# Attention rows from a v formed once, with blocks of p as the stationary operand

## The chip, the cores and the metric

The kernel runs on one core of a Trainium2 chip, alone. The metric is device time in microseconds (us) of one launch, as a median over runs. All data are float32.

Engines are called as the profile calls them: PE is TensorE (matrix multiply; PEld its weight loads), DVE is VectorE, ACT is ScalarE, POOL is GpSimd, SP is SyncE, which here only issues DMAs. A matmul has a stationary operand, loaded into the array as weights of 128 rows by up to 128 columns, and a moving operand that is streamed through; its result goes to PSUM, of which a bank holds 512 float32 per partition. A float32 matmul appears in the profile as two records.

## The reference, cut to what matters

Two layers over N = 4096 rows. Layer 0 is attention over all rows (width D = 512) with the matrix `adj` added twice to the scores, layer 1 a graph convolution with the same `adj` (hidden width 128). Each is followed by a residual and a layer norm.

```python
q, k, v = x @ Wq.T + bq, x @ Wk.T + bk, x @ Wv.T + bv
a = q @ k.T / sqrt(512) + adj + adj
x1 = layernorm(x + softmax(a) @ v)
h = relu(adj @ (x1 @ W1) + b1)
out = layernorm(x1 + adj @ (h @ W2) + b2)
```

The change concerns `softmax(a) @ v` alone. Because the rows of the softmax sum to one, `softmax(a) @ v = softmax(a) @ (x @ Wv.T) + bv`, which can be computed as `(p @ x) @ Wv.T` or as `p @ (x @ Wv.T)`, p being the exponentials, divided by their row sums at the end.

## The kernel before

The work is laid out by hand: `tc.manual_schedule()` keeps each engine's instructions in the order in which the Python code issues them. Rows of the attention are handled in 8 groups of 512 (`NG`, index g). The scores are held transposed: for group g a tile pair q (16 of them) holds 256 keys by 512 rows of the group.

**Small recursion.** Most products of 512x512 blocks use the Strassen-Winograd form: 7 products of half-sized blocks, in the order 1, 2, 6, 7, 5, 4, 3 (`ORDER`), of sums and differences of quarters (S1 to S4 on one side, T1 to T4 on the other). Products 1, 6, 5, 3 accumulate in one PSUM bank (X), 2, 7, 4 in another (Y), and after each product the bank is read and added to a quarter of the result. So reads are many and small, and a product must not be added to a bank before the previous sum there has been read.

**Stages.**
- Start: M, the product of Wq and Wk, is formed, and u = M x for group 0 (`u_fast(0)`).
- Scores of group 0 (`qk`, read by `qk_read`), with `u_fast` of groups 1 to 7 placed between. Beside them `sum_x` loads x by pairs of tiles, lets GpSimd form four sums of its quarters and stores them in `xs_d`.
- Groups: while `qk` forms the scores of group g+1, the exponentials p of group g are prepared and multiplied with x. This is `px`: for each of 5 blocks of tile pairs (2, 2, 4, 4, 4 pairs) 7 products, called phases.
- Then the convolution (`strassen`, line 1028, and the loop at line 1330) and the output rows.

**Order.** A group of scores is 16 units (`NP`) of 7 steps. In a step TensorE gets two matmuls of `qk` (call them k, j with j = 0 or 1; X and Y have one buffer each, tags "x" and "y"), then `qk_read` if j = 1, then items from the list `todo` as far as their planned microseconds are due. Before all that, the hooks of the step run: `at(unit, step, f)`. A group's px begins near unit `s1 = (g + 1) * NP`, when its scores are complete:

- `turn_max` (s1, step 5) and `spread_max` (s1+1, step 1) give the maximum of each row in every partition (`MB`); `new_max` has accumulated it on VectorE;
- `shift` subtracts it (VectorE, two per pair), `exps` takes the exponential (ScalarE), `px_t2` forms two differences (GpSimd), all at the places listed in `PREP`;
- `sums` adds the exponentials to `LACC` on GpSimd, two adds of 128x512 per pair; `row_sums` turns this by TensorE and reduces it;
- `px_items`: stationary is a block of x (or of its stored sums), moving the quarter of p, 256 columns. Both 128-row halves f of a phase share a bank. During phase 6 `px_t34`, during phase 7 `px_t1` change the quarters of p in place on VectorE. `px_read` adds the bank to `OT`;
- banks of px, u and v come from four buffers with the tag "o"; the stationary x comes from a ring of four buffers `XN`, loaded by `load_x` three phases ahead.

`OT` is (p x) transposed. `row_items(g - 1)` begins in unit s1+1 and places, between the first px items of group g, the row work of group g-1: `rows_out_fast` (28 matmuls with Wv by the 7 products; the last group has `rows_out`, 16 matmuls of 512 columns, placed beside the convolution), then the layer norm (`stats`, `rows_norm`), `project` and `project2` (x1 @ W1 into `t_sb`) and `add_b2` (x1 + b2 to `x1_d`).

Of the kernel before, what the change touches and what calls it, by code (L numbers as in the profile page):

```python
# [18 lines left out]
P = 128  # L19
# [5 lines left out]
def tile_graph_attention_then_gcn(  # L25
# [89 lines left out]
    xs_d = {a: dram.tile([P, 4, b - a, 2 * P], F32, name=f"xs_d{a}") for a, b in BLOCKS}  # L115
# [38 lines left out]
    FAST_V = range(NG - 1)  # L154
    QUARTER = {1: (0, 0), 2: (0, 0), 6: (1, 0), 7: (1, 1), 5: (1, 1), 4: (1, 0), 3: (0, 1)}
    L = {}
    MV, owing = {}, []
    UT, UO, XTS, SA, S, XN, CB, MB, MACC, LACC, O, OT, RL, XR, T = ({} for _ in range(15))
# [158 lines left out]
    def sum_x(q):  # L317

        if q % 5 < 3:
            w = t_sb[:, ts(q % 5, 8), :].rearrange("p (a b) c -> p a (b c)", a=4)  # L320
        else:
            w = xnp.tile([P, 4, 2 * P], F32, tag="xn", name=f"w{q}")
        a11, a21, a12, a22 = (w[:, k] for k in range(4))
        nc.sync.dma_start(
            w.rearrange("p (t a) c -> p t (a c)", t=2),
            x[ts(q // 2, W), :].rearrange("(t j p) d -> j p t d", p=P, t=2)[q % 2],
        )

        def row_part(r):
            if q >= PER // 2:  # L330
                row_parts(q // 2 * PER + q % 2 + 2 * r, w[:, 2 * r : 2 * r + 2].rearrange("p a d -> p (a d)"))

        def add():
            tt = nc.gpsimd.tensor_tensor
            tt(a22, a21, a22, ALU.add)
            tt(a21, a21, a11, ALU.subtract)
            tt(a11, a22, a11, ALU.subtract)
            tt(a12, a12, a11, ALU.subtract)

        def store():  # L340
            a = max(a for a, _ in BLOCKS if a <= q)
            nc.gpsimd.dma_start(xs_d[a][:, :, q - a, :], w)

        T["sum_x", q] = row_part, add, store
# [111 lines left out]
    def sums(g, q):  # L456
        ck = pair(g, q)
        if q == 0:
            LACC[g] = accp.tile([P, W], F32, tag="lacc", name=f"lacc{g}")
            nc.gpsimd.tensor_tensor(LACC[g], ck[:, 0, :], ck[:, 1, :], ALU.add)  # L460
        else:
            for h in range(2):
                nc.gpsimd.tensor_tensor(LACC[g], LACC[g], ck[:, h, :], ALU.add)  # L463


    PHASES = [(g, a, b, k) for g in range(NG) for a, b in BLOCKS for k in ORDER]

    def load_x(n):
        g, a, b, k = PHASES[n]
        pool = xnp2 if n % 4 > 1 else xnp  # L470
        XN[n] = pool.tile([P, b - a, 2 * P], F32, tag="xn", name=f"xn{n}")
        plain = {1: (0, 0), 2: (1, 0), 4: (1, 1)}
        if k in plain:
            t, f = plain[k]
            src = x.rearrange("(d t j p) f -> t p d j f", p=P, t=2, j=2)[t]
            for d in range(a // 2, b // 2):
                nc.sync.dma_start(
                    XN[n][:, 2 * d - a : 2 * d - a + 2], src[:, d, :, ts(f, 2 * P)]
                )
        else:  # L480
            nc.sync.dma_start(XN[n], xs_d[a][:, {6: 0, 7: 1, 3: 2, 5: 3}[k]])
# [24 lines left out]
    def px_read(g, first, k):  # L506

        letter = "PX" if k in (1, 6, 5, 3) else "PY"
        ps = T[letter].rearrange("p (f i) -> p f i", f=2)
        f, i = {1: (0, 0), 2: (0, 0), 6: (1, 0), 7: (1, 1), 5: (1, 1), 4: (1, 0), 3: (0, 1)}[k]  # L510
        to = OT[g][:, 2 * f : 2 * f + 2, ts(i, HW)]

        def go():
            if first and k in (1, 6, 7, 3):
                if g == NG - 1:
                    nc.vector.tensor_copy(to, ps)
                else:
                    nc.scalar.copy(to, ps)
            else:
                nc.vector.tensor_tensor(to, ps, to, ALU.add)  # L520

        px_reads.append((letter, go))
# [9 lines left out]
    def px_items(g):  # L532
        def one(n, q, f):
            _, a, b, k = PHASES[n]

            def go():
                if q == a and f == 0:
                    if n + 3 < len(PHASES):
                        load_x(n + 3)
                    if k in (6, 5, 3, 4):  # L540
                        read_px(("PY",) if k == 4 else ("PX",))
                    if k == 1 and a == 0:
                        OT[g] = rowp.tile([P, ND, W], F32, tag="ot", name=f"ot{g}")
                    if k in (1, 2, 7):
                        T["PX" if k == 1 else "PY"] = bank("o", f"p{n}", 4)
                begins = k in (1, 2, 7) and q == a
                nc.tensor.matmul(  # L547
                    T["PX" if k in (1, 6, 5, 3) else "PY"][:, ts(f, HW)],
                    XN[n][:, q - a, ts(f, P)],
                    quarters(g, q)[{1: 0, 2: 2, 6: 1, 7: 0, 5: 1, 4: 2, 3: 3}[k]],  # L550
                    start=begins and f == 0,
# [3 lines left out]
                if f == 1:  # L555
                    if k == 6:
                        px_t34(g, q)
                    if k == 7:
                        px_t1(g, q)
                    if q == b - 1:  # L560
                        px_read(g, a == 0, k)
# [4 lines left out]
            one(n, q, f)  # L566
            for n, (g_, a, b, k) in enumerate(PHASES)
            if g_ == g
            for q in range(a, b)
            for f in range(2)  # L570
        ]

    def row_sums(g):
        ps = turn(LACC[g], f"l{g}")
        l = small.tile([P, PER], F32, tag="l", name=f"l{g}")
        nc.vector.tensor_reduce(l, ps, AX.X, ALU.add)
        RL[g] = small.tile([P, PER], F32, tag="rl", name=f"rl{g}")
        if g in FAST_V:
            L[g] = l
            nc.vector.scalar_tensor_tensor(RL[g], l, EPS, l, ALU.mult, ALU.mult)  # L580
        else:
            nc.vector.reciprocal(RL[g], l)

    def add_bv(g):
        xr = XR[g]
        for r in range(PER):
            nc.gpsimd.tensor_tensor(xr[:, r, :], xr[:, r, :], bv_t, ALU.add)
            if g in FAST_V:
                nc.scalar.activation(
                    xr[:, r, :], xr[:, r, :], AF.Copy, scale=L[g][:, r : r + 1]  # L590
                )
# [24 lines left out]
    def rows_out(g, r, c):  # L616
        if c == 0 and r == 0:
            read_px()
        if c == 0:
            T["ro"] = mbank(f"x1_{g}_{r}")  # L620
        ps = T["ro"]
        nc.tensor.matmul(  # L622
            ps, OT[g][:, c, ts(r, P)], wv_t[:, c, :], start=c == 0, stop=c == ND - 1
        )
        if c == ND - 1:
            xr = XR[g][:, r, :]
            nc.vector.scalar_tensor_tensor(xr, ps, RL[g][:, r : r + 1], xr, ALU.mult, ALU.add)
            T["norm", g, r] = norm_stats(small, xr)

    def rows_out_fast(g, k, j):  # L630

        ot = OT[g].rearrange("p (f c) (h i) -> p f h c i", f=2, h=2)
        a11, a12, a21, a22 = (ot[:, f, h] for h in range(2) for f in range(2))
        tt = nc.vector.tensor_tensor

        sum_ = (nc.gpsimd if g == NG - 2 else nc.vector).tensor_tensor

        def read(k):  # L640
            ps = T["VX" if k in (1, 6, 5, 3) else "VY"].rearrange("p (j o) -> p j o", j=2)
            h, i = QUARTER[k]
            to = XR[g][:, 2 * h : 2 * h + 2, ts(i, HW)]
            tt(to, ps, to, ALU.add)

        def stats(r):

            mv = small.tile([P, 4], F32, tag="mv", name="mv2").rearrange("p (n s) -> p n s", n=2)
            for n in range(2):
                st = small.tile([P, nc.vector.BN_STATS_DIM], F32, tag="stats", name="stats")  # L650
                nc.vector.bn_stats(st, XR[g][:, r + n, :])
                nc.vector.bn_aggr(mv[:, n], st)
            rstd = small.tile([P, 2], F32, tag="rstd", name="rstd2")
            tt = nc.gpsimd.tensor_tensor
            tt(rstd, mv[:, :, 1], RL[g][:, r : r + 2], ALU.add)
            tt(rstd, rstd, half_t.to_broadcast([P, 2]), ALU.pow)
            sh = small.tile([P, 2], F32, tag="shift", name="shift2")
            tt(sh, mv[:, :, 0], rstd, ALU.mult)
            nc.gpsimd.tensor_scalar(sh, sh, -1.0, None, ALU.mult)
            for n in range(2):  # L660
                T["norm", g, r + n] = sh[:, n : n + 1], rstd[:, n : n + 1]

        if (k, j) == (1, 0):
            read_px()
            T["s3"] = rowp.tile([P, 2, HW], F32, tag="x1t", name=f"s3_{g}")
            sum_(T["s3"], a11, a21, ALU.subtract)
            sum_(a21, a21, a22, ALU.add)
        if j == 0 and k in (1, 2, 7):
            if k != 1 and m_tags[0] == T["v tag"]:
                m_tags.reverse()  # L670
            T["VX" if k == 1 else "VY"] = mbank(f"v{g}_{k}")
            if k == 1:
                T["v tag"] = m_tags[-1]
# [711 lines left out]
```

## Time and profile before

| | us |
|---|---|
| runs | 2302.60, 2301.88, 2300.53 |
| median | 2301.88 |
| span of the profiled execution, first to last instruction | 2301.7 |
| the same execution's busy PE / DVE / POOL / ACT | 2273.5 / 1615.5 / 1016.0 / 402.8 |
| start of `qk` of group 0, and of the first px | 38, 244 |
| start of the last group's px stage, and of the convolution | 1714, 1849 |

The profile is of one execution; its span is the time of the run but for a fraction of a microsecond, so sums are made against 2301.7. [...]

### The profile page before, as it was taken

To read this page: it belongs to the slowest core of one execution; us is meant where nothing else is said; L and a number is where in the kernel's file an instruction comes from. 1 tells how busy PE (TensorE), PEld (TensorE's weight loads), DVE (VectorE), ACT (ScalarE), POOL (GpSimd) and SP (SyncE) were. 2 spreads that over 40 slices of the span, in tenths; PEclk is the share of its full clock that TensorE was granted. 3 is DMA by queue.
4 is the path that set the end of the run, shared out by engine and by line. 5 is a ranking of instruction groups with operands and counts; after the bars stand their busy time and mean duration, and the time that the engine had idled before them with its cause. 6 is when DMAs were issued, how large, how long until landed. Compare 5 with 4: busy or idle time off the path is not lost.

```text
span 2301.7 us, 28624 instructions
## 1 busy us (share of the span) xinstructions
PE 2273.5 (99%) x10744; PEld 1766.8 (77%) x10744; DVE 1615.5 (70%) x2287; ACT 402.8 (18%) x442; POOL 1016.0 (44%) x1007
## 2 busy tenths in 40 slices
PE   9999999999999999999999999999999999999998
PEld 7888788888888888888888888888887843333456
DVE  5676676676667657866776687567657877888864
ACT  2212211131122113111311121122112000000012
POOL 2666454184337425631653274237428830001043
PEclk9999999999999999999999999999999999999999
DMA  6899778567847694777578477947754468999996
GB/s 189 282 308 296 218 220 232 176 189 212 245 132 215 187 256 110 217 210 217 151 215 241 142 214 196 256 117 210 199 185 156 160 240 325 333 347 374 353 382 218
DMA packets 283721, 525.16 MB, mean 228 GB/s; under 512 B 23297, under 2 KB 130561, under 8 KB 282689
## 3 DMA queue, kind: packets, MB, share of 16 engines
q1 hardware_dynamic: 229040, 406.12, 52.2%
q0 software_dynamic: 43296, 103.56, 20.5%
q10 hardware_dynamic: 11248, 13.65, 1.9%
q8 instruction: 86, 1.41, 0.2%
q14 instruction: 51, 0.41, 0.1%
HBM read 475.27 MB, written 46.41 MB: 227 GB/s over the span
## 4 chain that ended last, share of the span: by engine, by line
PE 93%; DVE 3%; DMA 1%; POOL 1%; issue 0%; ACT 0%; POOLq 0%; DVEq 0%
PE p L547 31%; PE X L407 19%; PE b L1028 15%; PE Y L407 14%; PE psu L246 4%; PE v L676 3%; PE acce L1330 2%; PE tps L722 1%; PE ops L1284 1%; DVE s L497 1%; DVE s L502 1%; PE x1ps L713 1%; DMA s_d<-sa 1%; PE x L622 1%; DMA sa<-in_xT_dram 1%; PE psm L831 1%
## 5 line engine op out<-in xcount | busy, mean ns | idle before, releaser
L547 PE MATMUL p<-s,xn 128*128 128x256 f32 x3584 | 895.6, 380 | 6.7 <-DVE s L502 1.9
L547 PEld LDWEIGHTS p<-s,xn 128*128 128x128 f32 x3584 | 677.6, 190 | 108.4 <-DVE s L502 5.8
L407 PE MATMUL X<-ut,sa 128*128 128x256 f32 x1984 | 514.7, 383 | 3.2 <-DVE macc L429 2.2
L463 POOL TENSOR_TENSOR lacc<-lacc,s 128x512 f32<-128x512 f32 x240 | 345.3, 1439 | 204.7 <-ACT s L454 193.9
L407 PEld LDWEIGHTS X<-ut,sa 128*128 128x128 f32 x1984 | 371.1, 191 | 63.9 <-DVE s L420 14.0
L420 DVE TENSOR_TENSOR s<-X,s 128x512 f32<-128x512 f32 x256 | 176.4, 689 | 285.8 <-PE X L407 281.7
L407 PE MATMUL Y<-ut,sa 128*128 128x256 f32 x1408 | 362.1, 380 | 1.9 <-DMA sa<-in_xT_dram 1.9
L407 PEld LDWEIGHTS Y<-ut,sa 128*128 128x128 f32 x1408 | 267.5, 191 | 38.2 <-DVE s L450 2.3
L454 ACT ACTIVATE s<-s 128x1024 f32<-128x1024 f32 x128 | 135.4, 1058 | 794.6 <-DVE s L450 794.6
L429 DVE TENSOR_TENSOR macc<-macc,s 128x512 f32<-128x512 f32 x240 | 254.7, 1061 | 1.2
L420 DVE TENSOR_TENSOR s<-Y,s 128x512 f32<-128x512 f32 x192 | 131.9, 687 | 165.9 <-PE Y L407 165.0
L450 DVE TENSOR_TENSOR s<-s,mb 128x512 f32<-128x512 f32 x256 | 230.0, 907 | 0.7 <-ACT mb L370 0.7
L520 DVE TENSOR_TENSOR ot<-p,ot 128x512 f32<-128x512 f32 x248 | 168.9, 681 | 28.6 <-PE p L547 28.3
L356 POOL DMA_DIRECT2D s<-in_adjT_dram x64 | 84.3, 1317 | 231.9 <-ACT s L351 231.1
L995 DVE TENSOR_TENSOR tt<-ck 128x1024 f32<-128x1024 f32 x112 | 138.4, 1271 | 38.6 <-PE b L1028 32.9
L1028 PE MATMUL b<-tt,st 128*64 128x512 f32 (+1 forms) x768 | 156.1, 541 | 0.0
L351 ACT COPY s<-cb 128x2048 f32<-128x2048 f32 x64 | 121.0, 1891 | 50.7 <-PE p L547 39.8
L490 POOL TENSOR_TENSOR s<-s 128x256 f32<-128x256 f32 x128 | 121.4, 949 | 0.6
L1028 PEld LDWEIGHTS b<-tt,st 128*64 128x64 f32 x768 | 53.9, 137 | 87.8 <-issue 79.4
L491 POOL TENSOR_TENSOR s<-s 128x256 f32<-128x256 f32 x128 | 108.7, 849 | 10.0
L497 DVE TENSOR_TENSOR s<-s 128x512 f32<-128x512 f32 x128 | 112.9, 902 | 0.0
L460 POOL TENSOR_TENSOR lacc<-s 128x512 f32<-128x512 f32 x8 | 10.6, 1323 | 203.4 <-ACT s L454 203.4
(191 smaller groups left out, 2129.3 us busy)
## 6 DMA issues: line engine op xcount, KB each, us to landing
ck<-in_adjT_dram SPq DMA_DIRECT2D x128, 1024.0 KB, 7.4
s<-in_adjT_dram POOLq DMA_DIRECT2D x64, 1024.0 KB, 11.6
sa<-s_d SPq DMA_DIRECT2D x224, 256.0 KB, 5.4
xn<-in_x_dram SPq DMA_DIRECT2D x192, 256.0 KB, 4.5
xn<-xs_d SPq DMA_DIRECT2D x96, 512.0 KB, 5.2
sa<-in_xT_dram SPq DMA_DIRECT2D x168, 256.0 KB, 4.6
xn<-xs_d SPq DMA_DIRECT2D x64, 256.0 KB, 4.0
ut<-u_d SPq DMA_DIRECT2D x49, 256.0 KB, 7.0
```

The costliest lines, as they stand in the source:

```text
L407: nc.tensor.matmul(T["X" if k in (1, 6, 5, 3) else "Y"][:, ts(j, HW)], SA[g, d, a][:, c, j, :], UT[g, b][:, c, :], start=k in (1, 2, 7) an ...
L420: nc.vector.tensor_tensor(ck, ps, ck, ALU.add)
L429: nc.vector.tensor_tensor(MACC[g], MACC[g], ck[:, h, :], ALU.max)
L450: nc.vector.tensor_tensor(ck, ck, MB[g], ALU.subtract)
L454: nc.scalar.activation(ck, ck, AF.Exp, scale=2.0)
L463: nc.gpsimd.tensor_tensor(LACC[g], LACC[g], ck[:, h, :], ALU.add)
L490: nc.gpsimd.tensor_tensor(b12, b12, b11, ALU.subtract)
L497: nc.vector.tensor_tensor(b, b, t2, ALU.subtract)
L520: nc.vector.tensor_tensor(to, ps, to, ALU.add)
L547: nc.tensor.matmul(T["PX" if k in (1, 6, 5, 3) else "PY"][:, ts(f, HW)], XN[n][:, q - a, ts(f, P)], quarters(g, q)[{1: 0, 2: 2, 6: 1, 7: 0 ...
L995: nc.vector.tensor_tensor(t[:, :2], v[:, :, 1], v[:, 0], ALU.subtract)
L1028: nc.tensor.matmul(BK[n][k][ts(half, HH)], lhs, right(u, i, half, b), start=q == 0, stop=q == NP - 1,)
```

## The change

v = x Wv^T is formed once for all 4096 rows, beside the scores of group 0, and its 7 quarter combinations are stored in DRAM (`vs_d`). In px the blocks of p become the stationary operand, and v streams, 256 columns and a 257th that holds a constant (1, -1, 2 or 0, as the seven products need), which yields the row sums of p in the same products. The result is no longer transposed and needs no product with Wv. Gone are `sums`, `row_sums`, `rows_out`, `rows_out_fast`, the sums of x, and the scaling of x by the row sums. Row work of group g-1 (`rows_sum`, `rows_stats`, `rows_norm`) stands in hooks, and px of a group begins one unit later.

```diff
+    def v_fast(d):
...
+                for c in range(2):
+                    nc.tensor.matmul(
+                        X["X" if k in (1, 6, 5, 3) else "Y"][:, ts(j, HW)],
+                        SA[0, d, OPERANDS[k][0]][:, c, j, :],
+                        WV[OPERANDS[k][1]][:, c, :],
...
+    def store_v(d):
+        to = v_place(d)
+        nc.scalar.dma_start(to[:, 0], VW[d][:, 0])
+        nc.scalar.dma_start(to[:, 1:3], VW[d][:, 2:4])
+
+    def sum_v(d):
+        a11, a21, a12, a22 = (VW[d][:, k] for k in range(4))
+        tt = nc.gpsimd.tensor_tensor
+        tt(a22, a21, a22, ALU.add)
+        tt(a21, a21, a11, ALU.subtract)
+        tt(a11, a22, a11, ALU.subtract)
+        tt(a12, a12, a11, ALU.subtract)
+
+    def store_sums(d):
+        nc.gpsimd.dma_start(v_place(d)[:, 3:7], VW[d])
...
     def load_x(n):
         g, a, b, k = PHASES[n]
         pool = xnp2 if n % 4 > 1 else xnp
...
+        XN[n] = pool.tile(
+            [P, b - a, HW + 1], F32, tag="xn", name=f"xn{n}", padded_shape=[P, 4, HW + 1]
+        )
+        place, ones = {1: (0, 1.0), 2: (1, 1.0), 4: (2, 0.0), 6: (3, -1.0), 7: (4, -1.0),
+                       3: (5, 2.0), 5: (6, 0.0)}[k]
+        nc.gpsimd.memset(XN[n][:, :, HW:], ones)
+        nc.sync.dma_start(XN[n][:, :, :HW], vs_d[a][:, place])
...
-        def one(n, q, f):
+        def one(n, r, q):
...
+                    if k in (1, 2):
+                        T[letter, r] = bank("o", f"p{n}_{r}", 4)
                 nc.tensor.matmul(
-                    T["PX" if k in (1, 6, 5, 3) else "PY"][:, ts(f, HW)],
-                    XN[n][:, q - a, ts(f, P)],
-                    quarters(g, q)[{1: 0, 2: 2, 6: 1, 7: 0, 5: 1, 4: 2, 3: 3}[k]],
-                    start=begins and f == 0,
+                    T[letter, r][:, : HW + 1],
+                    quarters(g, q)[{1: 0, 2: 2, 6: 1, 7: 0, 5: 1, 4: 2, 3: 3}[k]][:, ts(r, P)],
+                    XN[n][:, q - a, :],
+                    start=k in (1, 2, 7) and q == a,
...
-            for q in range(a, b)
-            for f in range(2)
+            for r in range(2)
+            for q in range(a, b)
...
+    def rows_sum(g, r):
...
+        if r == 0:
             read_px()
...
+            RL[g] = small.tile([P, PER], F32, tag="rl", name=f"rl{g}")
+            nc.vector.reciprocal(RL[g], OT[g][:, :, 0, HW])
+        for n in range(2):
+            xr = XR[g][:, r + n, :].rearrange("p (f c) -> p f c", f=2)
+            nc.vector.scalar_tensor_tensor(
+                xr, OT[g][:, r + n, :, :HW], RL[g][:, r + n : r + n + 1], xr, ALU.mult, ALU.add
+            )
...
+    def rows_stats(g, r):
+
+        mv = small.tile([P, 4], F32, tag="mv", name="mv2").rearrange("p (n s) -> p n s", n=2)
+        for n in range(2):
+            st = small.tile([P, nc.vector.BN_STATS_DIM], F32, tag="stats", name="stats")
+            nc.vector.bn_stats(st, XR[g][:, r + n, :])
+            nc.vector.bn_aggr(mv[:, n], st)
+        rstd = small.tile([P, 2], F32, tag="rstd", name="rstd2")
+        tt = nc.gpsimd.tensor_tensor
+        nc.gpsimd.tensor_scalar(rstd, mv[:, :, 1], EPS, None, ALU.add)
+        tt(rstd, rstd, half_t.to_broadcast([P, 2]), ALU.pow)
...
         return [
...
+            *w(4), *pro(0), *w(4), *pro(1), *w(2),
+            *pro2(0), *w(2), *pro(2), *w(2), *pro2(1), *w(2), *pro(3), *w(2), *pro2(2), *w(4),
...
-    work[1] = 15, [(0.86, f) for g in range(1, NG) for f in u_fast(g)] + [(0, lambda: owing.pop()())] * 2
+    first = []
+    for d in range(NG):
+        if d:
+            first += [(0.86, f) for f in u_fast(d)]
+        late = [(0.86, f) for f in v_fast(d)]
+        if d:
+            late[4:4] = [(0, lambda d=d: sum_v(d - 1))]
+            late[12:12] = [(0, lambda d=d: store_sums(d - 1))]
+        first += late
...
+    work[1] = NP - 1, first
...
     PREP = [
-        (1, LATE), (2, EARLY), (2, LATE), (3, MID), (4, EARLY), (4, LATE), (5, EARLY), (5, LATE),
+        (1, (2, 3, 4)), (1, (4, 5, 6)), (2, LATE), (3, MID), (4, EARLY), (4, LATE), (5, EARLY), (5, LATE),
...
-            at(s1 + unit, n2, sums, g, q)
             at(s1 + unit, n2, px_t2, g, q)
...
             items = row_items(g - 1, lambda n: [px.pop() for _ in range(n * by)])
-            work[s1 + 1] = NP, items + px[::-1]
-        else:
-            work[s1 + 2] = NP - 1, px
+            px = items + px[::-1]
+            for n in range(4):
+                at(s1 + 1, 3 + n, (rows_sum, rows_stats)[n // 2], g - 1, n % 2 * 2)
+                at(s1 + 2, n, rows_norm, g - 1, n)
+        work[s1 + 2] = NP - 1, px
```

## Prediction

> **What bounds the kernel now.** I read the engine shares first, then the chain that ended last, then one stretch of the middle.
>
> ```profile
> PE 2273.5 (99%) x10744; PEld 1766.8 (77%) x10744; DVE 1615.5 (70%) x2287; ACT 402.8 (18%) x442; POOL 1016.0 (44%) x1007
> ...
> PE 93%; DVE 3%; DMA 1%; POOL 1%; issue 0%; ACT 0%; POOLq 0%; DVEq 0%
> ```
>
> ```profile
> 650.00:850.00 200.00, 199.63 (x948) 174.42 (x947) 141.72 (x201) 42.16 (x41) 98.27 (x91) 1.00 0.71 197
> ```
>
> TensorE is full: 199.6 of 200 us in the middle, and 93% of the chain. VectorE (141.7) and GpSimd (98.3) have room on the average. So work taken off GpSimd (the row sums) is worth nothing directly; what counts is the sum of matmuls and every new place where TensorE waits. From the chain in order of time:
>
> ```profile
> 1080.74 1.73 PE v L676 x8
> ...
> 1294.73 1.73 PE v L676 x8
> ...
> 1852.67 3.63 PE x L622 x8
> ```
>
> Eight records are four matmuls of 256 columns: 0.216 us a record, 0.432 a matmul. The first two rows open `rows_out_fast` of neighbouring groups, so a group lasts 214.0 us. Its matmuls: 224 of qk and 224 of px, 96.8 each, 28 of v, 12.1, project and project2 5.7, three turns 1.3: 212.7. Barely 1.3 is lost to waits.
>
> **The matmuls.** Removed: `rows_out_fast`, 7 x 28 x 0.432 = 84.7; `rows_out` of the last group, 4 x 3.63 = 14.5; eight turns for row sums at 0.44, 3.5. Added: `v_fast`, 8 x 28 x 0.432 = 96.8; one more column in 1792 px matmuls, 774 x 1/256 = 3.0. The sum is -2.9: v is formed in one place instead of eight, not saved. By stages: the first group's scores grow by 96.8, each middle group shrinks by 12.3, the end by 15. Swapping which px operand is stationary costs nothing: as many weight loads of 128 columns (190 ns each, beside the matmuls) as before.
>
> **The first stage.** Scores of group 0 take 181 us of TensorE now, 278 after. Hidden below that: the load of Wv on SP (1 MB, 7.7 us to landing now; issued ahead of the u matmuls that begin at 26 us, used from 44); 32 GpSimd sums of 512 columns for 64 of 256; copies by ScalarE (18% busy) and its two stores of each block, which wait for a VectorE add of 0.68, with only the next copies behind them; GpSimd's store of the sums. 14.7 MB are stored instead of 8.4, but over a longer stretch (DMA share 0.96 from 60 to 250 us now). TensorE loses some 5 us at 224 to 243 us to late `sa` loads and a full queue; with DMA less dense I take -2, bounds -8 and +3.
>
> **The moved rows, where I expect the loss.** Before, row work of group g-1 lay between v matmuls in the unit that starts px of group g. After, px starts a unit later, and in that unit (s1+1) TensorE has only seven steps of qk, while `rows_sum` and `rows_stats` put all their VectorE work at steps 3 to 6, ahead of the qk reads of the same steps. Bank X is single: product 1 of the next block can't start until product 3 has been read. That such a read holds TensorE shows already in the scores before the first px:
>
> ```profile
> 237.16 3.22 PE Y L407 x8
> 240.38 2.17 PE X L407 x8
> ...
> 242.57 0.70 DVE s L420
> 243.28 0.04 issue
> 243.32 1.13 PE X L407 x4
> ```
>
> X starts 0.05 us after its read has ended. VectorE's prices come from its timeline:
>
> ```profile
> 1313.36 0.70 DVE L651 BATCH_NORM_STATS2 stats<-xr 128x6 f32<-128x512 f32 x1
> 1314.09 0.18 DVE L652 BATCH_NORM_AGGREGATE mv<-stats 128x2 f32<-128x6 f32 x1
> 1314.18 0.66 DVE L651 BATCH_NORM_STATS2 stats<-xr 128x6 f32<-128x512 f32 x1
> 1314.88 0.18 DVE L652 BATCH_NORM_AGGREGATE mv<-stats 128x2 f32<-128x6 f32 x1
> 1314.98 0.66 DVE L450 TENSOR_TENSOR s<-s,mb 128x512 f32<-128x512 f32 x1
> 1315.56 0.68 DVE L420 TENSOR_TENSOR s<-X,s 128x512 f32<-128x512 f32 x1
> 1316.16 0.68 DVE L644 TENSOR_TENSOR xr<-v,xr 128x512 f32<-128x512 f32 x1
> ```
>
> From start to start a read or shift takes 0.60, statistics of one row tile 0.81. A scaled add took 0.75 (the four of line 627), so 0.67 from start to start; a reciprocal took 0.18. From the read of product 5 to the end of the read of product 3 VectorE's order after the change is: read, shift, reciprocal, two scaled adds, shift, two scaled adds, read, shift, four statistics, read: 0.60 + 0.60 + 0.18 + 1.34 + 0.60 + 1.34 + 0.60 + 0.60 + 3.24 + 0.69 = 9.8 us. TensorE has products 4 and 3 in that time, 8 matmuls, 3.5 us. With 0.2 allowed for handing over twice it idles 9.8 + 0.2 - 3.5 = 6.5. Nothing behind it can pass: the next product 1 stands ahead of px in TensorE's order.
>
> Two things add to it. One is GpSimd: ops with two SBUF operands take a mean of 907 ns (L450) against a median of 683, so 0.22 each is lost beside GpSimd; with its row sums gone I take half, 7 ops x 0.11 = 0.8. The other is the clock. A gap of 1.9 us stood before the row at 237.16 above, which then took 3.22 where 1.73 is normal; the granted clock (third figure from the end) fell in that stretch:
>
> ```profile
> 238.00:242.00 4.00, 4.00 (x13) 3.23 (x12) 1.29 (x2) 0.26 (x1) 2.47 (x3) 0.61 1.08 361
> ```
>
> With the row behind it, some 1.7 us were lost. That gives 6.5 + 0.8 + 1.7 = 9.0 for each crowded unit. Six groups have one beside qk (1 to 6): +54. Bounds per unit: 5 (steps partly covered, no clock loss) and 12.5 (full contention and two slow clock windows), so 30 to 75.
>
> [...]
>
> **Ends of px phases.** px now runs a whole row half at a time in four banks, all in use, where two of four were free. `px_t34` of a tile stands closer to its use. In the second block of two tiles, product 6 is followed at once by product 7: its second matmul is 0.43 us behind, while VectorE does a qk read (0.60), a px read (0.42, from the 128x256 form of line 1045) and px_t34 (0.60) first: about 1 us of wait. In blocks of four the same order leaves 2 us of slack. With the banks read a little late at block borders, 1.2 a group, 7 groups: +8, bounds 0 and 20. px reads double in number at 0.42 for 0.60: 5 us more VectorE work a group, under its 58 idle ones. Loads of v land in 1 KB pieces as those of x did (256 KB in 4.5 us), three phases ahead; the memset of the ones waits on GpSimd for the same buffer, and behind it stand `px_t2` and the accumulating loads, needed a unit later: hidden. The four GpSimd steps of `rows_stats` (0.60, 0.75, 0.27, 0.22) now stand ahead of `px_t2` of the second tile; its product 6 is 8 matmuls of px and as many of qk away, 7 us: hidden too, and a stall of 2 us if not.
>
> **The last group.** Without qk and v to cover the chain from maximum to first exp, px starts into about 8 us of gaps (turned maximum 0.59, two shifts 1.2, exp 1.06, then the same row work). Now the start of that stage loses some 7 with GpSimd's sums in the chain, and the rest 7. I take +4 with the clock, bounds 0 and 10.
>
> **Sum.** The profiled span is 2301.7; the median of the runs is 2301.88, so 0.2 lies around it. -2.9 - 2 + 54 + 8 + 4 = +61: **2363**. Low bounds: -3 - 8 + 30 + 0 + 0 = +19; high: -3 + 3 + 75 + 20 + 10 = +105.
>
> **Rivals.** (1) *Faster*: the crowded units are covered, because VectorE starts them ahead and finishes in TensorE's shadow. For it: VectorE is 70% busy and loses the row sums' interference. Then remain -3, at best -8 in the first stage, and half of the 14 idle us of the last stage now: 2301.7 - 3 - 8 - 7 + 8 = 2292. It decides where a crowded unit costs under 1.6 us; against it stands the 9.8 of VectorE against 3.5 of TensorE in fixed order.
> (2) *Slower still*: 257 columns cost more than 1/256. Rows show 0.111 us for 128, 0.216 for 256 and 0.430 for 512 columns, linear, but none is odd. If a record went up by a step of 16 columns, 13.5 ns x 3584 = 48 less the 3 counted: 2408.
> (3) *No change*: the units cost only what the first stage and the last give back, some 1.6 us each: 2292 + 6 x 1.6 = 2302.
>
> **Chances.** The forecast case 0.77, faster 0.09, 257 columns 0.10, no change 0.04. A difference of 0.2%, 4.6 us, is what measurement can tell. The range 2312 to 2407 takes in both bounds of the forecast case and the lower part of (2); it leaves out (1), (3) and the rest of (2). Faster 0.09, same 0.04, slower 0.87.
>
> **What would show it.** Right: six gaps of 5 to 12 us on TensorE, released by the qk read, a group apart, with a lower granted clock behind each; groups of about 212 us; the first px some 95 us later; px records still at 0.217. Wrong: groups near 201 us (no crowding), px records above 0.220, or gaps released by DMA or GpSimd.

## The result, and the profile after

The changed kernel takes 2393.14 us (median of 4 runs, 2389.43 to 2393.18), the kernel before on the same chip 2302.24 (4 runs): a ratio of 1.0391, 95% interval 1.0376 to 1.0406. The profiled execution took 2393.18 us, its span is 2391.4. The forecast was 2363, range 2312 to 2407: the sign and the main cause held, the size fell 30 us short.

From the page of the changed kernel, the engine shares, the chain that ended last and one group of instructions (the count of records, then busy us and mean ns of one record, then idle time ahead and its releasers):

```profile
PE 2296.3 (96%) x10736; PEld 1788.0 (75%) x10736; DVE 1510.3 (63%) x2510; ACT 403.5 (17%) x474; POOL 648.0 (27%) x991
...
PE 20%; DVE 2%; POOL 1%; issue 1%; POOLq 0%; DVEq 0%
...
L444 PE MATMUL X<-ut,sa 128*128 128x256 f32 x1984 | 521.7, 387 | 51.6 <-DVE s L457 51.6
```

Records overlap: in the same profile eight of 256 columns take 1.89 us from the first start to the last end (X at 750.24), and 0.216 from start to start. VectorE lost 105 us of work and GpSimd 368, and the span grew by 90: neither was the limit. TensorE's share fell from 99% to 96%. The chain, 93% TensorE before, is followed here for only about a quarter of the span, so it says nothing of the middle; the waits do. TensorE's waits (line, releaser, us in total, times, longest):

```profile
PE X L444 <- DVE s L457: 51.6, 9, 7.4
PE p L571 <- DVE s L520: 15.5, 10, 2.2
...
PE b L997 <- DVE tt L968: 4.1, 1, 4.1
PE p L571 <- POOL xn L503: 3.7, 3, 2.0
```

The first is the crowded unit: the qk matmuls of bank X wait for `qk_read`, longest 7.4. The second is a px product waiting for `px_t34`. The third lies in the convolution, the fourth, mostly for a memset of the ones, in the last px stage. In the timeline of TensorE (start, us, engine and line, in brackets the idle time before and its releaser) the large gap comes back group by group:

```profile
544.39 2.08 PE L444 MATMUL X<-ut,sa 128*128 128x256 f32 x4 [7.44 <-DVE s L457]
...
759.55 2.07 PE L444 MATMUL X<-ut,sa 128*128 128x256 f32 x4 [7.43 <-DVE s L457]
...
974.65 2.08 PE L444 MATMUL X<-ut,sa 128*128 128x256 f32 x4 [7.43 <-DVE s L457]
```

The rows are 215.1 us apart, where a group took 213.9 to 214.5 before. VectorE's timeline ahead of the second row is the order that the prediction wrote out:

```profile
749.32 0.68 DVE L487 TENSOR_TENSOR s<-s,mb 128x512 f32<-128x512 f32 x1
749.92 0.17 DVE L631 RECIPROCAL rl<-ot 128x4 f32<-128x4 f32 x1
750.18 1.41 DVE L634 SCALAR_TENSOR_TENSOR xr<-ot,rl,xr 128x512 f32<-128x512 f32 x2
751.51 1.22 DVE L487 TENSOR_TENSOR s<-s,mb 128x512 f32<-128x512 f32 x1
752.65 1.87 DVE L634 SCALAR_TENSOR_TENSOR xr<-ot,rl,xr 128x512 f32<-128x512 f32 x2
754.44 0.68 DVE L457 TENSOR_TENSOR s<-Y,s 128x512 f32<-128x512 f32 x1
...
758.84 0.66 DVE L457 TENSOR_TENSOR s<-X,s 128x512 f32<-128x512 f32 x1
759.53 0.75 DVE L464 TENSOR_TENSOR macc<-s 128x512 f32<-128x512 f32 x1
```

The read of Y, whose matmuls ended by 750.4, starts at 754.44; shift and statistics stand before the read of X at 758.84, and product 1 starts at 759.55, 0.05 after that read's end. The row at 759.55 lasts 2.07 for 4 records instead of 1.03. The granted clock (third figure from the end) shows why; windows around that gap and around the second gap of the same kind:

```profile
751.00:754.20 3.20, 1.13 (x6) 0.65 (x4) 3.20 (x4) 0.10 (x1) 2.04 (x2) 1.00 0.72 254
754.30:764.50 10.20, 4.95 (x12) 3.93 (x13) 5.81 (x13) 2.95 (x4) 4.51 (x11) 0.50 0.00 1
764.60:768.00 3.40, 3.40 (x20) 2.98 (x19) 1.29 (x2) 1.81 (x4) 0.10 (x1) 1.00 0.25 76
590.50:593.80 3.30, 1.15 (x6) 0.69 (x5) 3.30 (x5) 1.06 (x1) 2.29 (x5) 1.00 1.10 248
593.90:597.20 3.30, 3.30 (x9) 2.66 (x8) 2.97 (x6) 0.00 (x0) 1.06 (x1) 0.50 0.78 290
```

The clock is at half from 754.3 to 764.5, of which TensorE works from 759.55 on: some 2.5 us lost. After the second gap, 2.15 us at 591, it is at half for 3.4 us more: 1.7 lost.

By stages, cut at the transposes that spread each group's maximum (`spread_max`) and at the last px product; the forecast column puts the prediction's terms to the stage in which each falls:

| stretch | before | after | difference | forecast |
|---|---|---|---|---|
| start to the maximum of group 0 | 232.5 | 331.7 | +99.2 | +94.8 |
| to the maximum of group 1 | 204.5 | 199.5 | -5.0 | +1 |
| the next five groups | 1070.8 | 1075.4 | +4.7 | -10.5 |
| to the maximum of group 7 | 207.9 | 208.0 | +0.1 | -2 |
| last px stage | 131.5 | 127.9 | -3.6 | -8 |
| convolution and output | 454.6 | 448.9 | -5.7 | -15 |
| sum | 2301.7 | 2391.4 | +89.7 | +60.3 |

### The profile page after: what moved, and what is told of

Same layout as the page of the kernel before. It is cut to its first block, busy times and chain, and to the rows that moved or that the text cites. A ratio compares the mean times of both kernels' runs of the same rounds, so it can differ in the third digit from the quotient of the medians.

```text
span 2391.4 us, 29110 instructions
## 1 busy us (share of the span) xinstructions
PE 2296.3 (96%) x10736; PEld 1788.0 (75%) x10736; DVE 1510.3 (63%) x2510; ACT 403.5 (17%) x474; POOL 648.0 (27%) x991
## 3 DMA queue, kind: packets, MB, share of 16 engines
q8 instruction: 86, 1.41, 0.2%
## 5 line engine op out<-in xcount | busy, mean ns | idle before, releaser
L571 PE MATMUL p<-xn,s 128*128 128x257 f32 x3584 | 918.8, 385 | 25.9 <-DVE s L520 15.5
L571 PEld LDWEIGHTS p<-xn,s 128*128 128x128 f32 x3584 | 685.7, 193 | 135.6 <-DVE s L520 20.5
L444 PE MATMUL X<-ut,sa 128*128 128x256 f32 x1984 | 521.7, 387 | 51.6 <-DVE s L457 51.6
L503 POOL MEMSET xn<- 128x4 f32 (+1 forms) x280 | 29.7, 109 | 755.9 <-PE p L571 707.7
L543 DVE TENSOR_TENSOR ot<-p,ot 128x257 f32<-128x257 f32 x496 | 204.4, 418 | 41.4 <-PE p L571 41.2
L487 DVE TENSOR_TENSOR s<-s,mb 128x512 f32<-128x512 f32 x256 | 198.9, 778 | 1.2 <-ACT mb L407 1.0
L466 DVE TENSOR_TENSOR macc<-macc,s 128x512 f32<-128x512 f32 x240 | 194.3, 809 | 0.6
L513 POOL TENSOR_TENSOR s<-s 128x256 f32<-128x256 f32 x128 | 109.0, 852 | 207.3 <-ACT s L491 206.6
L514 POOL TENSOR_TENSOR s<-s 128x256 f32<-128x256 f32 x128 | 109.4, 855 | 10.0
L520 DVE TENSOR_TENSOR s<-s 128x512 f32<-128x512 f32 x128 | 95.7, 787 | 0.0
L997 PE MATMUL b<-ck,t_sb 128*64 128x512 f32 x384 | 94.7, 595 | 0.0
```

The source lines that it names most:

```text
L444: nc.tensor.matmul(T["X" if k in (1, 6, 5, 3) else "Y"][:, ts(j, HW)], SA[g, d, a][:, c, j, :], UT[g, b][:, c, :], start=k in (1, 2, 7) an ...
L466: nc.vector.tensor_tensor(MACC[g], MACC[g], ck[:, h, :], ALU.max)
L487: nc.vector.tensor_tensor(ck, ck, MB[g], ALU.subtract)
L513: nc.gpsimd.tensor_tensor(b12, b12, b11, ALU.subtract)
L514: nc.gpsimd.tensor_tensor(b12, b22, b12, ALU.subtract)
L571: nc.tensor.matmul(T[letter, r][:, : HW + 1], quarters(g, q)[{1: 0, 2: 2, 6: 1, 7: 0, 5: 1, 4: 2, 3: 3}[k]][:, ts(r, P)], XN[n][:, q - a, ...
```

## Experiments

Each is an edit of the changed kernel; gains are against its 2393.14. The kernel before took 2303.5 to 2304.2 beside these runs, where it took 2302.2 beside the changed kernel, so a gain is known to some 2 us.

One stage varies by itself. The maximum of group 0 comes at 331.7 us in the profile of the changed kernel, and at 327.0 to 329.5 in the profiles of the six runs below that change nothing ahead of it. So 2 to 5 us of their gains don't come from the edit. Where it matters, the gain behind that point is given too; it is worked out from the spans of the profiled executions.

**The row work moved out of the crowded unit.**

```diff
-                at(s1 + 1, 3 + n, (rows_sum, rows_stats)[n // 2], g - 1, n % 2 * 2)
-                at(s1 + 2, n, rows_norm, g - 1, n)
+                unit, place = ((3, 1), (3, 5), (6, 1), (6, 5))[n]
+                at(s1 + unit, place, (rows_sum, rows_stats)[n // 2], g - 1, n % 2 * 2)
+                at(s1 + 7, n, rows_norm, g - 1, n)
...
-            *w(4), *pro(0), *w(4), *pro(1), *w(2),
+            *late, *pro(0), *w(4), *pro(1), *w(2),
```

> The changed kernel with the row work of group g-1 moved out of the crowded unit s1+1: the scaled adds to units s1+3 (steps 1 and 5), the statistics to s1+6 (steps 1 and 5), rows_norm to s1+7, project and what follows behind 100 px matmuls. The same instructions, other places. Theory (VectorE's order in that unit holds bank X): the gaps of 7.4 us before product 1 of the next block and the 10 us of half clock at each (2.6 us lost) vanish in the six middle groups, so 6 x 10 = 60 us less, about 2333; the 2.2 us gaps inside px stay. Where the moved work meets reads and px_t34, up to 1.5 a group comes back: 2333 to 2342. Rival (px's four banks or the loads of v set the period, and the gap only shows where it is): the idle time reappears elsewhere in the group, and less than 15 us is gained, 2378 or more.

Measured: 2330.67 us, 62.5 less (ratio to before 1.0118, 1.0103 to 1.0133); behind the maximum of group 0 59.6, the 60 of the theory. TensorE's waits:

```profile
PE p L571 <- DVE s L520: 11.4, 13, 1.0
PE X L444 <- DVE s L457: 11.2, 9, 3.3
```

The waits of bank X fell from 51.6 to 11.2 (the longest left is the one at 42 us, below), a middle group from 215.1 to 205.3 us, and the middle groups have no half clock any more. The theory holds; the rival asked for under 15. (The edit also drops the early px read and the assertion ahead of it in `rows_sum`. Here and in the run with both edits the convolution's sums of `t_sb` stand just ahead of the last projection of group 6, so they hold an older tile there; no instruction is added or left out, and the middle groups aren't touched.)

**`px_t34` and `px_t1` earlier.**

```diff
-                if r == 1:
+                if r == 0:
                     if k == 6:
                         px_t34(g, q)
```

> The changed kernel with px_t34 and px_t1 issued beside the first row half of a phase (r == 0) where they stood beside the second. Legal there, since the quarters that they write are read by later products alone. Theory (px_t34 of the second tile comes 0.43 us ahead of its use in the second block of two tiles, behind a read and a shift): the gap of 2.2 us there goes, and with it the 3.4 us of half clock behind it (1.7 lost): 7 x 3.9 = 27 us less, about 2366; the gaps of 7.4 us stay. Rival (the gap is contention with GpSimd's add beside it, or VectorE is simply late by then): the gap shrinks by less than 0.9, and under 10 us is gained, 2383 or more.

Measured: 2364.57 us, 28.6 less (1.0262, 1.0247 to 1.0277); behind the maximum of group 0 23.8, a little under the 27 of the theory. The waits for L520 fell from 15.5, longest 2.2, to 6.0, longest 1.0, in a middle group from 2.15 to 0.6, and no half clock follows them; the gap of 7.4 stayed. The theory holds but for that rest. The size of the gap has its reason on VectorE. Its timeline in the changed kernel, where the prediction had only a read, a px read and `px_t34` ahead of the product that starts at 593.32:

```profile
589.99 1.75 DVE L487 TENSOR_TENSOR s<-s,mb 128x512 f32<-128x512 f32 x1
591.66 0.68 DVE L457 TENSOR_TENSOR s<-X,s 128x512 f32<-128x512 f32 x1
592.26 0.41 DVE L543 TENSOR_TENSOR ot<-p,ot 128x257 f32<-128x257 f32 x1
592.59 0.68 DVE L520 TENSOR_TENSOR s<-s 128x512 f32<-128x512 f32 x1
```

A shift stands there too, and it took 1.75 where 0.68 is normal: GpSimd's `add_b2` ran beside it:

```profile
589.48 1.71 POOL L661 TENSOR_TENSOR xb<-xr,b_t 128x512 f32<-128x512 f32 x1
```

**Both.**

> Both of the edits above at once. Theory: the two gaps are separate, so the gains add: 60 + 27 = 87 less, about 2306, from 2302 to 2316, and a middle group takes 201 to 203 us, which is its 200.4 us of matmuls. Rival (VectorE or the banks have one common limit, and what one edit wins the other loses): clearly less than the sum of the two gains measured singly, by 15 us or more.

Measured: 2315.05 us, 78.1 less (1.0049, 1.0032 to 1.0066), inside the theory's 2302 to 2316 at its slow end; a middle group takes 202.8. The sum of the single gains is 91.1, so 13 are missing, just under the 15 that the rival asked for; behind the maximum of group 0 it is 83.4 against 75.9, so 7.5 are missing. They weren't separate: spreading the rows had already cut the px gap from 2.15 to about 1.0, without half clock behind it, since `add_b2` stands later there and the shift takes its 0.68.

**Half a dose: only the statistics moved** (to unit s1+3; the scaled adds stay in the crowded unit).

> Half a dose: of the row work only the statistics leave the crowded unit (to s1+3, rows_norm to s1+4, project behind 50 px matmuls); reciprocal and scaled adds stay in it. Theory: four statistics are 3.24 us of VectorE, so the gap of 7.4 falls to about 4.1. The matmuls lose 3.3 x 6 = 20 us; if the half clock behind the gap is as long as before, that is all (2373), if it goes in proportion another 7 (2366). Rival (the scaled adds' wait for the last px reads, or GpSimd's steps, end the gap): the gap stays above 6 and under 8 us is gained, 2385 or more.

Measured: 2374.71 us, 18.4 less (1.0308, 1.0293 to 1.0324), a little less than the 20 that the theory asked for at least. The gap itself is what VectorE's sum gives:

```profile
750.16 2.08 PE L444 MATMUL X<-ut,sa 128*128 128x256 f32 x4 [4.25 <-DVE s L457]
```

4.25 against 7.43 is 3.18 less for 3.24 us of statistics taken out. So the length of the gap goes with the VectorE work ahead of the read, one to one. The whole gained less than that, because waits came back elsewhere:

```profile
PE X L444 <- DVE s L457: 38.7, 15, 4.3
PE p L571 <- DVE s L520: 13.7, 16, 1.0
```

The px gap of 2.15 is gone from a middle group, with the half clock behind it, but three waits of 1.02, 0.85 and 1.17 stand in its place. In all such a group waits 7.3 us instead of 9.6 and loses 2.6 instead of 4.2 at half clock. That is 3.9; its period is 3.4 shorter.

**The convolution's rows alone.**

```diff
-        put((3, 4, 6, 8)[n], f, g, r)
+        put((20, 27, 34, 41)[n], f, g, r)
```

> The changed kernel with the last group's row work spread over the convolution: the px read stays at step 3, the scaled adds go from steps 3 and 4 to 20 and 27, the statistics from 6 and 8 to 34 and 41, the rest of the chain follows. Nothing else moves. Theory (VectorE did this work ahead of the sums of adjacency blocks that the next products wait for, and GpSimd's four add_b2 met the same sums): the gaps of 4.4, 2.8 and 0.8 us at 1951 to 1966 and two stretches of half clock of 3.4 us (1.7 lost in each) go, 9 to 13 us less, 2380 to 2384; the middle groups stay at 215.1. Rival (VectorE is about 80% busy in the convolution, so the same 10 us are missing wherever they stand): gaps of the same sum come back later, under 4 us gained.

Measured: 2383.48 us, 9.7 less (1.0345, 1.0331 to 1.0359), the lower end of the theory's range. But 2.3 of it lie ahead of the maximum of group 0; the convolution with the output takes 442.2 instead of 448.9, so the edit itself is worth some 6.7, less than the theory's 9 and more than the rival's 4. The wait of 4.1 for L968 is gone; the middle groups keep their gaps. That is the term which the prediction lacked. In the changed kernel VectorE put four statistics among the sums of adjacency blocks that TensorE needed next, and there `add_b2` met those sums. VectorE's timeline:

```profile
1957.43 2.35 DVE L964 TENSOR_TENSOR tt<-ck 128x1024 f32<-128x1024 f32 x2
1959.70 4.03 DVE L968 TENSOR_TENSOR tt<-ck,tt 128x512 f32<-128x512 f32 x2
1963.66 4.39 DVE L972 TENSOR_TENSOR ck<-ck,tt 128x512 f32<-128x512 f32 x2
...
1970.44 1.28 DVE L968 TENSOR_TENSOR tt<-ck,tt 128x512 f32<-128x512 f32 x2
```

Two adds that take 1.28 took 4.03 and 4.39 while GpSimd ran its four `add_b2`, 1958.7 to 1967.5.

**The load of Wv behind the first accumulating load.**

```diff
-    nc.sync.dma_start(
+    nc.gpsimd.dma_start(
         wv_t.rearrange("p f c h o -> p (f c) (h o)"), wvT.rearrange("(c p) o -> p c o", p=P)
     )
```

> The changed kernel with the load of Wv (1 MB) issued by GpSimd behind the first accumulating load of adjacency, where SP issued it ahead of it. Theory (the two share the DMA engines, so the accumulating load landed late and held the qk reads of the first unit): the gap of 2.5 to 4.1 us at 42 us goes, with the half clock that sometimes follows: 3 to 6 us less, 2387 to 2390. Against it: the differences of Wv are formed some 5 us later on GpSimd, and the second accumulating load is issued behind them, 1 to 2 us later. Rival (the accumulating load is slow by itself, or the wait only passes to the second one): a gap of 2 us or more stands at 42 us or at 50 to 56 us, and under 2 us is gained.

Measured: 2387.83 us, 5.3 less (1.0362, 1.0346 to 1.0378). In the changed kernel the first read of scores waits for the accumulating DMA, and TensorE for it, at half clock afterwards (8 records in 3.78 us where 1.89 is normal). VectorE's line and TensorE's:

```profile
45.49 0.69 DVE L457 TENSOR_TENSOR s<-X,s 128x512 f32<-128x512 f32 x1 [4.03 <-DMA s<-in_adjT_dram]
```

```profile
46.23 3.78 PE L444 MATMUL X<-ut,sa 128*128 128x256 f32 x8 [3.96 <-DVE s L457]
```

The first accumulating load took 8.4 us from issue to landing before, 15.0 in the changed kernel, 8.6 in this run. That holds throughout: 13.4 to 15.0 in the seven profiles with Wv's load ahead of it, 8.5 to 8.7 in the three with Wv's load behind. A gap of 1.8 is left at 43 us, so the rival has a small part of it. The maximum of group 0 comes at 326.3 instead of 331.7, against 327.0 to 331.7 in all seven: the edit is worth between 1 and 5 us.

Wv's own transfer does not explain it: in this run it went from 30.5 to 40.8, beside the accumulating load (29.6 to 38.2, on the same queue). The issues of SyncE show more, in the changed kernel and in this run:

```profile
26.81 0.37 SPq L815 DMA_DIRECT2D wv_t<-in_wvT_dram  x1
27.23 0.50 SPq L318 DMA_DIRECT2D w<-in_x_dram  x1
27.78 2.26 SPq L300 DMA_DIRECT2D s_d<-sa  x4
30.08 0.98 SPq L318 DMA_DIRECT2D w<-in_x_dram  x1
```

```profile
6.87 2.31 SPq L318 DMA_DIRECT2D w<-in_x_dram  x1
23.66 3.20 SPq L300 DMA_DIRECT2D s_d<-sa  x4
26.91 0.46 SPq L318 DMA_DIRECT2D w<-in_x_dram  x1
```

The issue of Wv's load had to wait until 26.81, and what stands behind it on SyncE waited too: two loads of x and four stores, 2 MB together. They landed between 34.8 and 45.2, beside the accumulating load (30.4 to 45.4); in this run all had landed by 30.6. That these late transfers slowed it fits the times; no run separates this from the move of Wv's load to another queue.

**GpSimd's adds out of the crowded unit.**

```diff
-        (1, (2, 3, 4)), (1, (4, 5, 6)), (2, LATE),
+        (1, (2, 3, 7)), (1, (4, 5, 8)), (2, LATE),
```

> The changed kernel with the four GpSimd adds of the first two tile pairs (px_t2) moved out of the crowded unit, to steps 0 and 1 of the next; VectorE's order stays. It asks what GpSimd's SBUF traffic adds to the pile. Theory: only the ops that run beside them are stretched (in the changed kernel's trace 1.22 for 0.68 and 1.87 for 1.41, 1.0 us together), so the gap of 7.4 falls to 6.4 to 6.8, and with six groups at most 6 us are gained. [...]

Measured: 2373.64 us in the one run, 19.5 less (16.5 behind the maximum of group 0). The gap is the theory's 6.4:

```profile
752.11 2.07 PE L444 MATMUL X<-ut,sa 128*128 128x256 f32 x4 [6.43 <-DVE s L457]
```

The gain is about three times what the theory allowed. It went through the clock: in five of the six groups the half clock around the gap lasts 6.8 us (748.2 to 755.0) where it lasted 10.2, and after the px gap there is none, though that gap is as long as before:

```profile
799.97 0.70 PE L571 MATMUL p<-xn,s 128*128 128x257 f32 x2 [2.15 <-DVE s L520]
```

```profile
796.00:799.30 3.30, 1.82 (x9) 1.26 (x7) 3.30 (x5) 0.88 (x1) 2.54 (x5) 1.00 1.12 214
799.50:802.70 3.20, 2.73 (x13) 2.42 (x14) 3.20 (x5) 0.00 (x0) 2.10 (x3) 1.00 1.05 345
```

A group takes 211.6 us, 3.4 less than 215.1: 1.0 of gap, 1.0 less at half clock behind it, and 1.7 at the px gap are 3.7, about that.

**All edits together**, with the two products that wait for adjacency blocks inside the last px stage a little later.

> All edits together: row work of the middle groups spread, px_t34 and px_t1 early, the last group's rows spread over the convolution, the load of Wv behind the accumulating load; besides, the products that wait for adjacency blocks inside the last px stage stand a little later (places 115 and 160 for 90 and 150), and the items of group 6 lie closer together in it. Theory: the spread and early edits gave 2315; the convolution gives 9 to 13 more, the first stage 3 to 5, the waits for adjacency blocks 3: 2294 to 2300, that is 0.2 to 0.4% below the kernel before, about the 2.9 us of matmuls that the change saves and what the first and last stages give back. Rival (a limit that the single edits have not met, of VectorE or the loads of v): 2305 or more, so the kernel before stays the faster.

Measured: 2299.84 us (11 runs, 2297.44 to 2301.37) against 2304.17: ratio 0.998, 0.9971 to 0.9988. So this version is faster than the kernel before, by about the 0.2% that can be told; the theory's range was met at its upper edge. TensorE's longest waits that are left:

```profile
PE X L444 <- DVE s L457: 7.4, 8, 1.9
PE p L571 <- ACT s L491: 4.3, 7, 0.6
...
PE p L571 <- issue: 3.1, 1, 3.1
PE p L571 <- POOL xn L503: 2.2, 1, 2.2
```

**Three edits more, on top of these.**

```diff
-        work[s1 + 2] = NP - 1, px
+        work[s1 + 2] = NP - (g == NG - 1), px
...
-    at(last_unit - 5, 0, lambda: [sum_t(0, 0, 8), sum_t(8, 8, 14)])
+    at(last_unit - 12, 0, sum_t, 0, 0, 8)
+    at(last_unit - 4, 0, sum_t, 8, 8, 14)
...
-        put(47 + 2 * r, add_b2, g, r)
+        put(47 + 7 * r, add_b2, g, r)
```

> All edits of the run e7_all and three more: px of the groups before the last runs on through unit s1+17 (16 units where it had 15), so that unit s1+1 has px matmuls between the qk products; GpSimd's sums of t_sb for the convolution stand in two places, 8 units apart; the four add_b2 of the last group stand 7 steps apart. Theory: in e7_all the one gap left in a middle group that is not a wait for the exponential is 0.95 us before product 1 in unit s1+1, since nothing stands between product 3 and its read; px matmuls cover it, 6 x 0.95 = 6 less; a wait of 2.2 for the memset of the ones behind GpSimd's eight sums, and one of 2.4 for VectorE beside add_b2, go: together 8 to 11 us, 2288 to 2292. Rival (tiles of scores are freed a unit later, and the next group's accumulating loads come late): gaps released by DMA, 2298 or more.

Measured: 2288.23 us (5 runs, 2287.89 to 2289.43) against 2303.48: ratio 0.9934, 0.9921 to 0.9948, the fastest of all, at the fast end of the theory's range. A middle group takes 202.0 instead of 202.8. The wait in unit s1+1, 0.78 in the run before rather than 0.95, fell to 0.35, and the one of 2.2 behind the sums is gone; one of 2.0 in the convolution stayed, and one of 3.6 for a load of v came in the last px stage, so the rival has that much.

## Why the prediction was right, and where it was off

- **Matmuls and operand swap: right.** 257 columns cost 0.217 us a record from start to start, so the rival with a step of 16 columns is refuted, and weight loads, 193 ns each after 190, don't show. With the rest mended, the last version has 11 us less TensorE busy time than the kernel before (2262.4 against 2273.5); 2.9 of that is the forecast sum, 1.7 is that it has one stretch of half clock where the kernel before had two around the end of group 0's scores, the rest I can't assign. One term was a little off: by its own parts (12.1 + 0.44 - 0.38) a middle group shrinks by 12.2 and not 12.3, which is why the forecast column adds up to 60 and the sum to 61.
- **Crowded unit: right in mechanism, order and place.** Six gaps, released by the qk read. The gap was put at 6.5 + 0.8 = 7.3 and measured 7.4. GpSimd's share, 0.8, measured 1.0 (the gap without its adds: 6.4). Only two of the four `px_t2` operations fell into the pile, and two of VectorE's rows were stretched, to 1.22 from 0.68 and to 1.87 from 1.41; in the convolution two adds took 4.0 instead of 1.28 beside `add_b2`. The clock was 1.7 in the sum and cost 2.5. Together 9.9 against 9.0; moving the work out gave 59.6 behind the maximum of group 0, against a term of 54; the 59.6 include part of the next point. Groups of 215 us, where 212 were forecast, are these two points together. No run shows the full contention that the upper bound of 12.5 allowed for; GpSimd's 1.0 and the 2.5 of the clock are what the runs showed in its place.
- **Ends of px phases: mis-sized.** The step "about 1 us of wait", 1.2 a group, left out a shift in VectorE's order and `add_b2` beside it. It cost 2.15 and 1.7 of half clock, 3.9 in each of six groups where 1.2 stood (0.2 in the first). Issuing `px_t34` early shows it: 23.8 us by itself, behind the maximum of group 0. This is the largest part of the error.
- **First stage: the wrong step is "Hidden below that: the load of Wv on SP".** Its own use was hidden; what its place in SyncE's order did to other transfers was not looked at. With it the accumulating load of the first scores took 15.0 us instead of 8.4: +99.2 in the profiled execution (+94.5 to +99.2 over seven profiles) instead of +94.8, and +93.0 to +93.9 in the three with the load behind.
- **End: not foreseen.** The prediction took -15 there for the products removed, and gave the moved row work only the start of the last px stage. In the convolution VectorE is busy 84% of the time (61% in a middle group), and spreading the same row work gave 6.7 there.
- **First px group: better than forecast** by 6. The kernel before lost 4.2 us to waits (the longest 1.9) and 1.7 to half clock there, the changed kernel 2.5 to waits and nothing to the clock; no experiment was made on it.
- **Faster was possible**, but by the edits of the order, not by the change as made: the 2292 of rival (1) was reached (2288) once the crowd was spread and the other edits were in.

## To carry to other kernels

Work that is moved must be placed against the operations that free single buffers: write out the fixed order of the engine from the last read to the next, compare it with what the matmuls last, and do so at each place to which the work goes, the last group included. A transfer that is itself hidden can still come with a delay of another that isn't: with Wv's load issued ahead, the first accumulating load took 15.0 us here, with it behind 8.6. A gap on TensorE cost its length and up to 3.1 us more through the clock here, depending on where it fell: the same 2.15 cost 3.9 in the changed kernel and 2.15 in the run with GpSimd's adds moved.

## What the runs showed of the hardware

**Half clock came in whole steps on a fixed grid.** In the trace's clock record every stretch of half clock that ends within the kernel lasts 3.41, 6.83 or 10.24 us (eight, two and six of them in the changed kernel, two of 3.41 in the kernel before), and within one run all of them start at whole multiples of 3.413 us from each other (in the changed kernel 145, 161, 208, 224 and 271 steps after the first). In the changed kernel 2.15 us without a matmul, all inside one step, was followed by half clock; in the run with GpSimd's adds moved, a gap of the same 2.15 was cut by a step's border, 1.6 to one side, and nothing followed. No sharp limit can be read: 1.9 us inside one step were followed by half clock in the kernel before (at 237.7), and 2.0 were not in the run with `px_t34` early (954.1 to 957.5).

**The period of the groups sat on that grid.** It was 215.04 us, 63 steps, in the changed kernel, and 211.63, 62 steps, both with the statistics moved and with GpSimd's adds moved, although these edits shorten the gap by 3.2 and by 1.0. So edits of different size gained the same 3.4; what they took from the waits of a group, 2.3 and 1.0, was made up for by 1.6 and 2.7 less at half clock. With `px_t34` early the distances were 62, 63, 62, 62 and 62 steps.

That the half clock, which ended at a step's border in these traces, pulls the groups onto the grid is argued from this. The distances of the groups' maxima speak for it. They close in on a whole number of steps: 215.17, 215.10, 215.07, 215.07 and 215.04 us in the changed kernel, 212.55, 212.09, 211.85, 211.76 and 211.67 with `px_t34` early. In the latter the gap stays at 7.4 throughout, while the time lost at half clock behind it falls from 3.1 to 2.2. With the row work spread, where the middle groups have no half clock, the distance is 205.3 from the first group on. No run shifts the groups against the grid and changes nothing else, so it is not shown.
